# A graph layer whose messages gather rows of a table: 249 of the gathers replaced by columns copied on VectorE and ScalarE

## The chip, the cores and the metric

The kernel runs on one core of a Trainium2 chip. A core has five engines with instruction streams of their own: TensorE (PE, with its weight loads shown apart as PEld), VectorE (DVE), ScalarE (ACT), GpSimd (POOL) and SyncE (SP). PE writes its products to PSUM; the other data lie in SBUF or in device memory, between which DMA moves them. The metric is the device time of one execution in microseconds (us); less is better.

## The reference, cut to what matters

There are 12,500 nodes with 96 features (`x`) and 412,500 edges, sorted by destination. Each edge makes a message from its two ends and its own four features; messages are normalised over all edges, summed by destination, and added to a node term; a layer norm ends it.

```python
def _mlp(h, W, b, gamma, beta):
    h = relu(h @ W + b)
    mu, var = h.mean(0), square(h - h.mean(0)).mean(0)
    return gamma * (h - mu) * rsqrt(var + EPS) + beta

node_feat = _mlp(x, W_node, b_node, g_node, beta_node)
edge_feat = _mlp(edge_attr, W_edge, b_edge, g_edge, beta_edge)
message = concatenate([x[row], x[col], edge_feat], axis=1)       # 412500 x 288
message = _mlp(message, W_msg, b_msg, g_msg, beta_msg)
agg = segment_sum(message, col, num_segments=12500)
out = layernorm(x + agg + node_feat)
```

`row` is `src`, in no order; `col` is `dst`, sorted.

## The kernel before

`x[row] @ W_msg[:96]` is a row of `x @ W_msg[:96]`. So the kernel first makes that table, `p_tab`, once for all nodes (`tables`), and another, `q_tab`, for the destinations. Edges are cut into 3223 tiles of 128; four tiles are a group (`GT`), four groups a block (`BG`). There are 806 groups in 202 blocks.

The rows of `p_tab` are fetched with indirect DMAs that Pool issues: one instruction for each tile, 128 rows of 96 floats (`gather`, L207). Pool's instructions, SP's and, in the main loop, those of all engines stand in the order in which the program is written.

First stage: tables, splitting of the edge features into three bf16 parts, their statistics (`edge_norm`, on PE, ACT and DVE), and the node term (`nodes`), whose result goes to DRAM (`y0_d`). `nodes` overwrites the transposed `x` in SBUF (`xp`, 96 partitions by 12,544 nodes, the tile `big`). Meanwhile Pool gathers the rows of the first 116 groups (`SPILL`), which are written to DRAM, and then those of the next 14 groups into a ring (`RING`). In three of the first groups SP fetches the last tile's rows itself, one by one (`early_rows`, `rows_of`): it loads 16 row numbers into registers (L457) and issues a DMA for each (L461).

Main loop: 806 steps, one group each (`for k in range(last)`). `plan` spreads the 29 spilled blocks among the 173 gathered ones; a spilled block is read back whole by SP (`fetch`). In step `k`:

- DVE, `message`: h = relu(z + gathered rows), L645, z being PE's product in PSUM;
- ACT, `squared`: squares of two groups' h, each second step, L659; DVE, `moments`: adds them up, L665;
- DVE: places of the destinations as ones and zeros (`places_of`, L653), and a finished block's sums into `agg` at an address from a register (`add`, L708 and L709); registers are loaded for eight blocks at once (L698);
- PE: sums by destination (`sums`, L689), edge products for the next block (`edges`, L614), and z for the group two steps on (`linear`, L628); ACT, `prepare`: the edge products' relu, L622;
- Pool, `ahead_of`: the gathers of the group 14 ahead, four instructions, where the step's group is a gathered one;
- SP: loads for the block two ahead (`load`, `fetch`), and in steps 64 to 112 the 13 parts of the node term, back into `big` (`residual`).

For the first four blocks rows of `x` itself are gathered, and PE multiplies them (`transposed`, L633). After the loop the sums are normalised and the output made (`output`).

Of the kernel before, what the change touches and what calls it, by code (L numbers as in the profile page):

```python
# [13 lines left out]
F32 = mybir.dt.float32  # L14
BF16 = mybir.dt.bfloat16
I32 = mybir.dt.int32
U8 = mybir.dt.uint8
# [9 lines left out]
P = 128  # L27
# [36 lines left out]
RING = 14  # L64
# [7 lines left out]
CL, CE = 3, 1  # L72
BUSY = 5
# [34 lines left out]
def gnn(ctx, tc, t):  # L108
# [8 lines left out]
    lin_d = dram.tile([len(FETCHED), P], I32, name="lin_d")  # L117
    stack_d = dram.tile([HI + PLACES * BG, RL], BF16, name="stack_d")
# [5 lines left out]
    rpool = ExitStack()  # L124
    nc.sync.dma_start(src_raw, t["src"][:, :RAW * BG * GT])
    ring = rpool.enter_context(tc.tile_pool(name="ring", bufs=RING // 2))
# [90 lines left out]
    def blocks():  # L217

        waiting = []
        for b in range(SPILL // BG + BEHIND):  # L220
            if b < SPILL // BG:
                for i in range(0, BG, 2):
                    pg = ring.tile([P, 2, GT, C], F32, name="pg")
# [45 lines left out]
    with tc.tile_pool(name="win", bufs=1) as win, tc.tile_pool(name="win_ps", bufs=2, space=PSUM) as ps:  # L269
# [8 lines left out]
        nc.sync.dma_start(lin_d, lins)  # L278
        by_block = "p (b g) t -> p b (g t)"
# [202 lines left out]

    order, steps = plan()

    def fast(ring):
        y0s, pair = [], [None]

        def ahead_of(g):
            if g % 2 == 0:
                pair[0] = ring.tile([P, 2, GT, C], F32, name="pg")  # L490
            if g < NG:
                return gather(g, pair[0][:, g % 2, :, :])

        with tc.manual_schedule(engines={ET.SP, ET.Pool}):
# [9 lines left out]
            with tc.tile_pool(name="nd", bufs=1) as nd, tc.tile_pool(name="nd_ps", bufs=2, space=PSUM) as nd_ps, \  # L504
                    tc.tile_pool(name="er", bufs=2) as er, tc.tile_pool(name="es", bufs=2) as es, \
                    tc.tile_pool(name="es1", bufs=1) as es1, tc.tile_pool(name="es_ps", bufs=3, space=PSUM) as es_ps:
                node, n, extra = nodes(nd, nd_ps), 7, early_rows(er)
                for i, _ in enumerate(edge_norm(es, es1, es_ps)):
                    next(node, None)
                    if i:  # L510
                        next(extra, None)
                    while 16 * i + 150 >= 20 * n:
                        next(store, None)
                        n += 1
                for x in (node, store, extra):
                    for _ in x:
                        pass
            got = {g: ahead_of(g) for g in range(SPILL, SPILL + RING)}
        with tc.tile_pool(name="fix", bufs=1) as fix, tc.tile_pool(name="msg", bufs=2) as work, \
# [75 lines left out]

            def transposed(k):
# [27 lines left out]
            def linear(k):  # L624
                s, g = steps[k]
                n = min(GT, NT - g * GT)
                for i in range(n):
# [3 lines left out]
                                     stop=g not in raw)  # L631
# [82 lines left out]
            with tc.manual_schedule(engines={ET.SP, ET.Pool, ET.PE, ET.DVE, ET.Activation}):  # L714
# [13 lines left out]
                for k in range(last):  # L728
# [33 lines left out]
                    if k >= 64 and k % 4 == 0 and loads:  # L762
                        y0s.append(residual(loads.pop(0)))
# [223 lines left out]
    y0s, bad = fast(ring)  # L987
# [5 lines left out]
    rpool.close()  # L993
# [60 lines left out]
```

## Time and profile before

| | |
|---|---|
| median of 3 runs | 4123.67 us (4118.46 to 4125.99) |
| the profiled execution | 4123.06 us |
| its span in the profile | 4121.3 us |
| busy share PE, PEld, DVE, ACT, POOL | 64%, 54%, 38%, 27%, 75% |
| gathers (L207) | 3156 + 64, first at 3.1 us, last at 4056.4 us |
| first h of the main loop | 665.4 us |
| granted TensorE clock, mean | 0.675 |

The profile records one execution. The busy shares are means over the span; a group row gives operation, operands, shapes, count, busy time, mean duration of one, and the idle time ahead of it with what ended it. "issue" is time in which an engine waited for nothing that the profile shows. A row with a q behind the engine's name (DVEq, SPq) is an instruction that the engine's sequencer handles itself, such as the load of registers or an issued DMA. A source row gives the shortest, the median and the longest duration in ns.

### The profile page before, as it was taken

The numbers are of one execution on the slowest core, as the hardware profiler recorded it, in microseconds if no ns is written. First come the engines' busy times: TensorE is split into PE (matmuls) and PEld (weight loads), VectorE is DVE, ScalarE is ACT, GpSimd is POOL, SyncE is SP. The second block draws the span as 40 slices with busy tenths as digits, with TensorE's granted clock in tenths as the row PEclk, the third lists the DMA queues.
The fourth block names the chain that finished last, engine by engine and source line by source line (L and its number), as shares of the span: only waits on it lengthen the run. The fifth ranks groups of instructions, "written<-read, shape, count | busy, mean of one in ns | idle before, by whom it ended". The sixth has DMA issues, their size and how long they took to land.

```text
span 4121.3 us, 43082 instructions
## 1 busy us (share of the span) xinstructions
PE 2632.2 (64%) x14949; PEld 2244.2 (54%) x15169; DVE 1584.5 (38%) x3051; ACT 1123.0 (27%) x1226; POOL 3092.1 (75%) x3248
## 2 busy tenths in 40 slices
PE   4256665666666666666666666666666666666667
PEld 3012324565666656556655566655565565666656
DVE  2499995333333233322333333333233333333323
ACT  1477882222222222212222222222122222222212
POOL 7777777777777777777777777777777777777774
PEclk7667886767766666656667666666666666666665
DMA  8855662223222222222222222222222222222222
GB/s 234 279 140 123 165 161 62 60 70 77 72 50 55 59 57 58 59 54 58 56 58 58 59 47 57 60 58 55 58 59 55 58 60 56 50 59 57 58 45 64
DMA packets 214865, 317.20 MB, mean 77 GB/s; under 512 B 126498, under 2 KB 132988, under 8 KB 211808
## 3 DMA queue, kind: packets, MB, share of 16 engines
q0 software_dynamic: 103040, 158.48, 19.2%
q1 hardware_dynamic: 98635, 150.92, 12.3%
q10 hardware_dynamic: 12960, 4.93, 0.5%
q8 instruction: 122, 2.00, 0.2%
q14 instruction: 108, 0.88, 0.1%
HBM read 258.19 MB, written 55.89 MB: 76 GB/s over the span
## 4 chain that ended last, share of the span: by engine, by line
POOL 50%; issue 22%; DVE 13%; DMA 10%; PE 4%; ACT 1%; SPq 0%; POOLq 0%; another core or an unknown queue 0%; DVEq 0%; ACTq 0%
POOL pg L207 50%; DMA pg<-p_tab,src 9%; DVE estats L419 9%; PE z L628 1%; PE py L971 1%; PE pa L689 1%; DVE mixed L665 1%; DMA x<-in_ea 0%; DVE part L424 0%; DVE h L645 0%; PE pn L358 0%; DVE nstats L360 0%; DVE big L369 0%; DVE y0s L388 0%; DVE agg L394 0%
## 5 line engine op out<-in xcount | busy, mean ns | idle before, releaser
L207 POOL DMA_INDIRECT pg<-p_tab,src x3156 | 3009.5, 954 | 964.7 <-issue 919.7
L628 PE MATMUL z<-rhs,left 128*128 128x96 f32 x6446 | 1276.3, 361 | 1099.9 <-DVE h L645 1092.3
L628 PEld LDWEIGHTS z<-rhs,left 128*128 128x128 f32 x6446 | 1166.7, 267 | 1304.9 <-DVE h L645 1271.9
L645 DVE CUSTOM_DVE_ANT_0 h<-z,pg 128x384 f32<-128x384 f32 x690 | 384.1, 557 | 2301.7 <-DMA pg<-p_tab,src 2244.6
L659 ACT ACTIVATE sq<-h 128x768 f32<-128x768 f32 x404 | 339.8, 841 | 2586.6 <-DVE h L645 2577.5
L689 PE MATMUL pa<-at,h 128*97 128x80 f32 x6446 | 940.5, 307 | 4.9 <-DVE h L645 4.9
L689 PEld LDWEIGHTS pa<-at,h 128*97 128x97 f32 x6446 | 889.4, 227 | 5.9 <-DVE h L645 5.9
L665 DVE TENSOR_TENSOR mixed<-mixed,sq 128x384 f32<-128x384 f32 x802 | 449.8, 561 | 13.9
L622 ACT ACTIVATE left<-pr 127x1024 f32<-127x1024 f32 x403 | 406.8, 1009 | 90.1 <-PE pr L614 60.8
L413 PE MATMUL pr<-ea,wide 128*128 128x512 bf16 x590 | 225.5, 476 | 213.7 <-ACT r L417 135.8
L419 DVE BATCH_NORM_STATS2 estats<-r 128x6 f32<-128x512 f32 x606 | 360.9, 676 | 0.0
L417 ACT ACTIVATE r<-pr 128x1024 f32<-128x1024 f32 x303 | 307.4, 1024 | 93.0 <-DVE estats L419 65.2
L413 PEld LDWEIGHTS <-wide 128*128 128x128 bf16 x606 | 68.8, 114 | 345.9 <-issue 326.1
L614 PE MATMUL pr<-late,we 128*128 128x512 bf16 x515 | 240.6, 530 | 19.2 <-DVE at L653 15.5
L653 DVE TENSOR_TENSOR at<-rel,mixed 128x496 f32<-128x496 bf16 x202 | 135.2, 669 | 6.8
L614 PEld LDWEIGHTS <-we 128*128 128x128 bf16 x806 | 108.4, 144 | 25.2 <-issue 24.7
L207 POOL DMA_INDIRECT pg<-in_x,src_raw x64 | 60.8, 950 | 20.7 <-issue 19.2
L386 PEld LDWEIGHTS pn<-center,big 96*128 96x128 f32 x196 | 42.4, 277 | 33.0 <-DVE y0s L388 22.9
L645 DVE CUSTOM_DVE_ANT_0 h<-z,pb 128x384 f32<-128x384 f32 x100 | 52.5, 548 | 13.6 <-PE z L628 13.5
L386 PE MATMUL pn<-center,big 96*128 96x96 f32 x196 | 41.9, 358 | 17.0 <-DVE y0s L388 16.3
L191 PE MATMUL pt<-w_msg,big 96*128 96x192 f32 x196 | 37.2, 357 | 17.2 <-ACT trow L195 11.7
L709 DVE TENSOR_TENSOR agg<-pa,agg 97x79 f32 x202 | 46.5, 230 | 0.0
(125 smaller groups left out, 658.2 us busy)
## 6 DMA issues: line engine op xcount, KB each, us to landing
pg<-p_tab,src POOLq DMA_INDIRECT x3156
pb<-spill SPq DMA_DIRECT2D x29, 768.0 KB
spill<-pg SPq DMA_DIRECT2D x55, 384.0 KB
ea<-stack_d SPq DMA_DIRECT2D x25, 480.0 KB
stack_d<-y SPq DMA_DIRECT2D x24, 448.0 KB
late<-stack_d SPq DMA_DIRECT2D x57, 180.0 KB
rhs<-q_tab SPq DMA_DIRECT2D x202, 46.5 KB
x<-in_ea SPq DMA_DIRECT2D x8, 896.0 KB
```

The lines of the kernel that those rows point to most:

```text
L207: made = [nc.gpsimd.indirect_dma_start(out=pg[:, i, :], out_offset=None, in_=tab[:, :], in_offset=bass.IndirectOffsetOnAxis(ap=idx[:, i:i ...
L413: nc.tensor.matmul(pr[:, k % 2, :], wide[:, P * i:P * (i + 1)], ea[:, b % J, :], start=True, stop=True)
L417: nc.scalar.activation(r, pr, AF.Relu)
L419: nc.vector.bn_stats(stats[:, (k - o) % NS, (k - o) // NS, :], r[:, 1 - o, :])
L614: nc.tensor.matmul(prs[s, half][:, i, :], we[:, 2 * half + i, :], block[s], start=True, stop=True)
L622: nc.scalar.activation(x[:C + WN, 2 * half:2 * half + n, :], pr[:C + WN, :n, :], AF.Relu)
L628: nc.tensor.matmul(zb[k % ZB][:, i * C:(i + 1) * C], left[s % 2][:KR, g % BG, i * P:(i + 1) * P], rhs[:KR, s % RB, g % BG, :], start=True, ...
L645: nc.vector._custom_dve(TENSOR_ADD_SAT, out=h[:, :n, :], in0=z, in1=rows[:, :n, :], s0=MOST, s1=0.0)
L653: nc.vector.tensor_tensor(to, rel[:, b:b + m, :].unsqueeze(3).to_broadcast([P, m, GT, WN]), nodes_of[:, :m].unsqueeze(2).to_broadcast([P, ...
L659: nc.scalar.activation(sq[:, :m, :n, :], hb[k // 2 % HP][:, k % 2:k % 2 + m, :n, :C], AF.Square)
L665: nc.vector.tensor_tensor(wide_sq, wide_sq, sq[:, i, :, :], op=OP.add)
L689: nc.tensor.matmul(by_place[s % 2][:C + 1, :NW], hb[k // 2 % HP][:r, k % 2, t, :], at[s % AB][:r, i, o + NW * t:o + NW * (t + 1)], start=i ...
```

## The change

For three in four of the pairs of gathered groups numbered 8 to 338 (249 pairs, `COPIED`), the last tile of the pair's second group is no longer gathered. Its 128 columns of the transposed `x` are copied, one by one, from `big` to a tile of 96 x 128 (`xcs`, six of them), and PE multiplies that with `W_msg[:96]` and adds it to z. The ring slot's part for that tile is set to zero once, so `message` is as it was.

A copy moves four bytes on each of 96 partitions, at an address from a register. Numbers of the columns, times four, are made in the first stage (`cols`, `col_d`), loaded by SP for four pairs at a time (`listed`), and loaded into registers 16 at a time, one portion ahead of their use (`places_at`). Of a pair's 128 columns ACT copies 64, 80 or 80, DVE the rest (`SHARES`). At the end of each step each of the two makes one or two portions, at most 12 steps ahead of their use (`Stream`).

For this, `big` must hold `x` until the last copy. The node stage runs at double pace, `x` is loaded anew behind it (`back`), and the 13 residual loads stand in the steps behind the last copy. The ring has 16 groups in place of 14, in tiles of its own rather than from a pool, and the scratch for Pool's descriptors is set to 8192 bytes.

```diff
-RING = 14
+RING = 16
+XB = 6
+TURN = 4
+AT_A_TIME = 16
+SHARES = (64, 80, 80)
+AHEAD_BY = 12
+RATE = 0.36
+LP = (NG - SPILL) // 2
+COPIED = [q for q in range(RING // 2, LP - 6) if q % TURN != TURN - 1]
...
         def ahead_of(g):
-            if g % 2 == 0:
-                pair[0] = ring.tile([P, 2, GT, C], F32, name="pg")
+            q = (g - SPILL) // 2
+            slot = ring[q % len(ring)]
+            without = int(g % 2 and q in COPIED)
+            if without and q % len(ring) not in zeroed:
+                zeroed.add(q % len(ring))
+                nc.vector.memset(slot[:, 1, GT - 1, :], 0.0)
             if g < NG:
-                return gather(g, pair[0][:, g % 2, :, :])
+                return gather(g, slot[:, g % 2, :, :], without)
...
                 for i, _ in enumerate(edge_norm(es, es1, es_ps)):
-                    next(node, None)
+                    for _ in range(2):
+                        next(node, None)
                     if i:
                         next(extra, None)
+                    if i > 14:
+                        for _ in range(min(3, len(homes))):
+                            back(homes.pop(0))
...
+            def places_at(j, lo, hi, engine):
+                q = COPIED[j]
+                _, val = nc.values_load_multi_w_load_instructions(
+                    numbers[q // TURN % 2][:, q % TURN, lo:hi], engines=[engine], min_val=0, max_val=4 * (N - 1),
...
+            def columns(j, lo, val, engine):
+                to = xcs[j % XB].bitcast(U8)
+                for i, x in enumerate(val):
+                    a, b = to[:, 4 * (lo + i):4 * (lo + i + 1)], places_in_x[:, bass.ds(x, 4)]
+                    if engine == ET.DVE:
+                        nc.vector.tensor_copy(a, b)
+                    else:
+                        nc.scalar.activation(a, b, AF.Copy)
+            class Stream:
...
+                    self.per = RATE * len(self.parts) / len(COPIED)
...
+                def step(self, k):
+                    self.due = min(self.due + self.per, self.per + 1)
+                    while self.due >= 1 and self.done < len(self.parts):
+                        j, lo, hi = self.parts[self.done]
+                        if COPIED[j] // TURN > loaded[-1] or uses[COPIED[j]] - k > AHEAD_BY or \
+                                (j >= XB and uses[COPIED[j - XB]] >= k):
+                            break
+                        val = self.next or places_at(j, lo, hi, self.engine)
+                        self.done += 1
+                        if self.done < len(self.parts) and self.at() // TURN <= loaded[-1]:
+                            self.next = places_at(*self.parts[self.done], self.engine)
+                        columns(j, lo, val, self.engine)
+                        self.due -= 1
...
             def linear(k):
...
+                    if i == GT - 1 and copied:
+                        nc.tensor.matmul(zb[k % ZB][:, i * C:(i + 1) * C], xcs[COPIED.index(q) % XB],
+                                         w_msg[:, 0, :], start=False, stop=True)
...
                     if g >= SPILL:
                         got[ahead] = ahead_of(ahead)
                         ahead += 1
-                    if k >= 64 and k % 4 == 0 and loads:
+                    listed()
+                    for x in streams:
+                        x.step(k)
+                    if all(x.done == len(x.parts) for x in streams) and loads:
                         y0s.append(residual(loads.pop(0)))
...
-    nc = bacc.Bacc("TRN2", target_bir_lowering=False, num_devices=1)
+    nc = bacc.Bacc("TRN2", target_bir_lowering=False, num_devices=1, dynamic_dma_scratch_size=8192)
```

Pool's gathers in the middle of the loop, before; `DMASW3` and the like are the eight semaphores of Pool's own DMAs, `DVE` is the release of a ring slot:

```order
L207 DMA pg<-p_tab,src 128x96 [waits DMASW5_49,DVE_49]
L207 DMA pg<-p_tab,src 128x96 [waits DMASW6_49]
L207 DMA pg<-p_tab,src 128x96 [waits DMASW7_49]
L207 DMA pg<-p_tab,src 128x96 [waits DMASW0_49]
L207 DMA pg<-p_tab,src 128x96 [waits DMASW1_49]
L207 DMA pg<-p_tab,src 128x96 [waits DMASW2_49]
L207 DMA pg<-p_tab,src 128x96 [waits DMASW3_49]
L207 DMA pg<-p_tab,src 128x96 [waits DMASW4_49]
L207 DMA pg<-p_tab,src 128x96 [waits DMASW5_49,DVE_49]
```

The same place of Pool's stream in the change (the line is now L215, the ring's slots are named `pg_75` to `pg_82`):

```order
L215 DMA pg_80<-p_tab,src 128x96 [waits DMASW3_49,DVE_49]
L215 DMA pg_80<-p_tab,src 128x96 [waits DMASW4_49]
L215 DMA pg_80<-p_tab,src 128x96 [waits DMASW5_49]
L215 DMA pg_80<-p_tab,src 128x96 [waits DMASW6_49]
L215 DMA pg_80<-p_tab,src 128x96 [waits DMASW7_49,DVE_49]
L215 DMA pg_80<-p_tab,src 128x96 [waits DMASW0_49]
L215 DMA pg_80<-p_tab,src 128x96 [waits DMASW1_49]
L215 DMA pg_81<-p_tab,src 128x96 [waits DMASW2_49,DVE_49]
```

A pair of groups has seven gathers in place of eight, and waits for DVE once a group rather than once a pair. Each gather still waits for the one eight before it.

ACT's stream in the main loop, before:

```order
L622 ACTIVATE left_4973<-pr 127x1024
L659 ACTIVATE sq<-h_4978 128x768
L622 ACTIVATE left_4972<-pr 127x1024
L659 ACTIVATE sq<-h_4976 128x768
L622 ACTIVATE left_4972<-pr 127x1024
```

And in the change, from the activation of one step (now L713) on (`REGISTER_ALU` adds a tile's address to a column's number; 16 such pairs of rows follow a load, and some steps have a second load and 16 more):

```order
L713 ACTIVATE left_4940<-pr 127x1024
L644 TENSOR_LOAD numbers_4976
L657 REGISTER_ALU
L657 ACTIVATE xc_4971<-big 96x4
L657 REGISTER_ALU
L657 ACTIVATE xc_4971<-big 96x4
```

The next activation of this kind stands behind 33 or 66 more instructions.

DVE's stream in the change, from the places of a block on (L749, before L653); the first four rows stand there before as well, and the next h follows them there:

```order
L749 TENSOR_TENSOR at_4949<-rel,mixed 128x4x4x31
L804 TENSOR_TENSOR total<-pa_4919,total 97x1
L805 ISA
L805 TENSOR_TENSOR agg<-pa_4919,agg 97x79
L644 TENSOR_LOAD numbers_4976
L655 REGISTER_ALU
L655 COPY xc_4970<-big 96x4
L655 REGISTER_ALU
L655 COPY xc_4970<-big 96x4
```

The load and its 16 additions and copies stand between a block's sums and the next group's h (L741).

More of the change, by code (lines that the diff above doesn't have):

```diff
@@ L222, in blocks @@
                 for i in range(0, BG, 2):
[L223 removed]
+                    pg = ring[(b * BG + i) // 2 % len(ring)]
                     for k in range(2):
@@ L517, in fast @@
                         pass
+                for i in homes:
+                    back(i)
             got = {g: ahead_of(g) for g in range(SPILL, SPILL + RING)}
@@ L596, in transposed @@
+            streams = [Stream(e) for e in (ET.Activation, ET.DVE)]
             def transposed(k):
@@ L625, in linear @@
                 s, g = steps[k]
+                q = (g - SPILL) // 2
+                copied = g >= SPILL and g % 2 and q in COPIED
                 n = min(GT, NT - g * GT)
```

45 lines of the change are left out of this document (38 added, 7 removed).

## The prediction

> **What bounds the kernel now.** I read the page's shares by engine first, then the busy time by window, then the groups and waits, and last the timeline. In the first fence stand a page's row, two windows (busy us and count for PE, PEld, DVE, ACT, POOL, then granted clock, DMA share, GB/s), the gathers' group, what Pool waited for, and the two largest waits.
>
> ```profile
> PE 2632.2 (64%) x14949; PEld 2244.2 (54%) x15169; DVE 1584.5 (38%) x3051; ACT 1123.0 (27%) x1226; POOL 3092.1 (75%) x3248
> ...
> 1000.00:2000.00 1000.00, 668.98 (x4000) 607.19 (x4060) 304.17 (x649) 211.19 (x238) 756.06 (x801) 0.66 0.26 59
> ...
> 750.00:4045.00 3295.00, 2178.37 (x13096) 1970.79 (x13290) 995.24 (x2122) 689.50 (x778) 2491.41 (x2637) 0.67 0.26 58
> ...
> L207 POOL DMA_INDIRECT pg<-p_tab,src x3156: 940/945/4104, 83.4 to 4056.4; - x198
> ...
>   DVE h L645: 4.3, 14
> ...
> ACT sq L659 <- DVE h L645: 2577.5, 395, 12.4
> DVE h L645 <- DMA pg<-p_tab,src: 2244.6, 617, 8.6
> ```
>
> Pool shows only 75% busy, but it is the bound: 801 gathers in 1000 us are one each 1.2484 us, 0.945 busy and 0.30 of issue, from the first windows to 4056.4. Its wait for a free ring slot (the DVE row) is 4.3 us in all, so it never stands still for the others. DVE waits 2245 us for gathered rows, and ACT 2578 us for DVE: both have time to spare, and so has PE (2178 of 3295 us). That the consumers could go much faster shows where the ring is still full, at the loop's start:
>
> ```profile
> 668.76 0.56 DVE L645 CUSTOM_DVE_ANT_0 h<-z,pg 128x384 f32<-128x384 f32 x1 [1.15 <-PE z L628]
> ...
> 677.26 0.56 DVE L645 CUSTOM_DVE_ANT_0 h<-z,pg 128x384 f32<-128x384 f32 x1 [1.41 <-PE z L628]
> ```
>
> Five groups lie between these rows, 1.7 us each, against 4 x 1.2484 = 5.0 us for a group's gathers.
>
> **The gathers removed.** There are 345 pairs of gathered groups; numbers 8 to 338 without each fourth are 249. One gather of the pair's eight goes: 249 x 1.2484 = **311 us** off Pool. The profiled execution took 4123.06 us, 1.8 more than its span of 4121.3 and 0.6 below the runs' median of 4123.67, so it stands for them. If all that is added stays hidden: 4123.06 - 311 = 3812.
>
> The copying lies in steps 3 to 783 of 806, by the program. These 781 steps have 781 x 690/806 = 669 gathered groups: 2674 gathers or 3338 us before, 2425 or **3027 us** after. What is added must fit into 3027 us, beside the present work of these engines. The window 750 to 4045 has 2637 gathers, 659 groups or 770 steps: per step 995.24/770 = 1.29 us of DVE, 0.90 of ACT, 2.83 of PE.
>
> **ScalarE's copies.** 18,592 copies in 1,162 portions of 16, each portion with a load of 16 registers and 16 register additions. The trace has no such copy, so its price comes from its parts.
>
> ```profile
> 130.72 1.79 ACT L359 ACTIVATE agg<-pn,vec 96x512 f32<-96x512 f32 x3
> ...
> L359 ACT ACTIVATE agg<-pn,vec 96x512 f32<-96x512 f32 x24 | 15.8, 679 | 49.4 <-PE pn L358 49.4
> ...
> L659 ACT ACTIVATE sq<-h 128x768 f32<-128x768 f32 x402 | 338.9, 843 | 2578.9 <-DVE h L645 2573.3 <-DVE h L643 5.5
> ...
> L659 ACT ACTIVATE sq<-h 128x384 f32<-128x384 f32 x1 | 0.5, 523 | 4.1 <-DVE h L645 4.1
> ```
>
> 843 - 523 ns for 384 elements more is 0.83 ns each, so 203 ns are fixed and four elements take 206. Three activations of 679 that need no wait take 1.79 us, so each overlaps the next by 0.12: about **0.09 us** from copy to copy on the engine. The sequencer ahead of it must make an addition and hand out an instruction for each:
>
> ```profile
> L715 ACTq TENSOR_LOAD <-flag x1: 473/473/473, 641.1 to 641.1; - x1
> L715 SPq TENSOR_LOAD <-flag x1: 722/722/722, 650.8 to 650.8; - x1
> ...
> L698 DVEq TENSOR_LOAD <-base_at x26: 541/598/612, 678.9 to 4059.2; - x26
> ...
> L572 SPq TENSOR_LOAD <-base_at x26: 708/776/806, 655.4 to 3959.9; - x26
> ...
> L457 SPq TENSOR_LOAD <-elin x24: 1165/1226/2637, 225.2 to 598.5; - x24
> ...
> 246.45 2.81 SPq L461 DMA_DIRECT2D erow<-p_tab  x9
> ...
> L461 SPq DMA_DIRECT2D erow<-p_tab x384: 221/228/398, 226.5 to 605.0; - x192
> ...
> L709 DVEq FUSED_REGOPS  x202: 69/69/79, 679.7 to 4063.3; - x101
> ```
>
> On SP nine transfers with a register step between them take 2.81 us, 9 x 0.228 of them their own: 0.094 us for a step and the next hand-out. The dearest row is DVE's, where one step of 69 ns and its hand-out make 0.14 (next fence), up to 0.15 with rounding. I take 0.10, nearer to SP's, since one plain addition is like SP's single move; bounds 0.094 and 0.15. A load of one register takes ACT 0.473; DVE's loads go from 541 ns (two, at the end) to 598 (eight), 9.5 ns a register, which makes 0.62 for sixteen; by SP's ratio of 1226 to 722 it is 0.80. I take 0.70.
>
> ACT's sequencer: 1162 x (0.70 + 1.60) = 2673, and some 40 for its 781 large activations: **2713 us**. Its engine: 781 x 0.90 + 18,592 x 0.09 = 2376. Both are under 3027. Whether they overlap or add is told by DVE, the first three rows without a load between L653 and L708, the others with one:
>
> ```profile
> 2032.82 0.67 DVE L653 TENSOR_TENSOR at<-rel,mixed 128x496 f32<-128x496 bf16 x1
> 2033.41 0.15 DVE L708 TENSOR_TENSOR total<-pa,total 97x1 f32<-97x1 f32 x1
> 2033.48 0.23 DVE L709 TENSOR_TENSOR agg<-pa,agg 97x79 f32 x1
> ...
> 2152.68 0.67 DVE L653 TENSOR_TENSOR at<-rel,mixed 128x496 f32<-128x496 bf16 x1
> 2153.38 0.16 DVE L708 TENSOR_TENSOR total<-pa,total 97x1 f32<-97x1 f32 x1
> 2153.52 0.24 DVE L709 TENSOR_TENSOR agg<-pa,agg 97x79 f32 x1
> ```
>
> A load of 0.598 us delays L708 by only 0.11 when it is made while L653 runs: the sequencer works ahead of its engine. With that lead L709 follows in 0.07 us, without it in 0.14. In the changed order each large operation has a load right behind it, so about one load a step is covered. Only with no overlap at all would ACT need 699 + 2673 = 3372 us.
>
> **VectorE's copies.** 13,280 in 830 portions. Per copy I take 0.125 us on the sequencer, between SP's 0.094 and DVE's own 0.15 for a longer step; per load 0.8, half-way from 598 + 8 x 9.5 = 674 ns to 598 x 1226/776 = 945: 830 x (0.8 + 2.0) = 2324. The engine: 781 x 1.29 + 13,280 x 0.07 = 1937. At the dearest, 0.15 and 0.95, the sequencer takes 2781. All are under 3027; added up without overlap they would be 1007 + 2324 = 3331. A portion stands ahead of the next group's h (L645) and lasts some 2 us; h's readers are sums and squares, and behind them the ring slot's release, which the ring's slack of 16 groups x 5 us covers.
>
> **What the copies cost Pool.** The trace shows VectorE stopping a gather:
>
> ```profile
> 71.84 0.36 DVE L261 CAST part<-whole 128x384 bf16<-128x384 f32 x1 [14.99 <-DMA uses<-in_uses]
> 71.99 1.02 POOL L207 DMA_INDIRECT pg<-in_x,src_raw  x1 [0.30 <-issue]
> ...
> 644.12 1.35 DVE L533 COPY rhs<-w_e 96x1152 f32<-96x1152 f32 x1
> ...
> 645.21 0.95 POOL L207 DMA_INDIRECT pg<-p_tab,src  x1 [0.30 <-issue]
> ...
> 154.05 2.69 POOL L207 DMA_INDIRECT pg<-p_tab,src  x1 [0.30 <-issue]
> ...
> 153.89 2.02 DVE L309 TENSOR_TENSOR x<-x,y 128x1792 f32<-128x1792 f32 x1 [2.22 <-ACT y L308]
> ```
>
> The gather under L309 ends 0.83 us after it (156.74 and 155.91), the one under L261 0.81 after it; that under the copy L533 is not longer. So some DVE operations from SBUF to SBUF hold up the gather's early part until they end. If the new copies do so, a gather meets one in about 45% of the time (13,280 x 0.10 of 3027) and waits half of 0.1 us: 0.022 x 2425 = **55 us**. Bounds: 0 (as under L533), and 0.15 us for each gather that meets one, 164. I take 55, since L261 is the nearer row: a plain one-source operation with few elements.
>
> The Trainium skill's "VectorE: DVE Perf Modes" (What auto-detection actually checks) gives a copy within SBUF with an even count its two-port mode, and "SBUF — State Buffer" (SBUF: two separate sides) says that such an operation locks Pool out of the shared port for its whole length. L261 bears this out. By these pages every DVE copy here holds the port and the term is 55 or more; by L533's row alone it would be 0 and the sum 3812.
>
> **Edits at nothing.** PE gets 249 x 2 x 0.323 us = 161 us of products, 0.2 a step beside 2.83, where a step will have 3.9. Its new product waits for columns that are copied up to twelve steps ahead; behind it on PE stand sums and the next products, for which DVE's h waits, so late columns are rivals 1 and 2.
>
> ```profile
> L633 PE MATMUL z<-w_msg,xt 96*128 96x96 f32 x128 | 30.1, 323 | 6.8 <-ACT xt L604 6.8
> ...
> big<-in_xp SPq DMA_DIRECT2D x14, 336.0 KB
> ...
> big<-y_d SPq DMA_DIRECT2D x12, 384.0 KB
> ```
>
> The 14 transfers that bring x back (4.8 MB) and the doubled pace of the node stage lie in the stage before the loop, where DVE's statistics last and Pool goes on with its gathers; two more ring groups give that stage 10 us more before Pool would stand. The 13 residual loads (4.7 MB) move from steps 64 on to those behind the last copy, 20 steps or 78 us, at a DMA share of 0.26; what stands behind them on SP, the loads for two blocks ahead, has some 20 us to spare. The queue of SP gets a small load of numbers each eight groups and no wait longer than a step. Ring slots are now freed by group; the wait stays VectorE's. Together 3 us, bounds 0 and 25.
>
> **Sum:** 4123 - 311 + 55 + 3 = **3870 us**. Pool stays the bound: 3027 + 55 = 3082 us of gathers in the copying steps, against 2713 on ACT.
>
> **Rivals.**
> 1. *ScalarE becomes the bound, still a gain.* It needs more than (3082 - 40)/1162 = 2.62 us a portion: an addition and hand-out of over 0.12 us. For it speaks DVE's 0.14, against it that ACT's load is shorter than both others' and SP's 0.094. At 0.12 with loads of 0.80, 1162 x 2.72 + 40 = 3201: 119 more than Pool, **3989**.
> 2. *ScalarE is the bound and the kernel slower than before.* The point is 3338 us of ACT: 2.84 a portion, 0.134 us per copy with loads of 0.70, or loads and copies that do not overlap with the large operations (3372). At DVE's 0.15 and 0.80 it is 1162 x 3.20 + 40 = 3758, 420 over: **4543**. Against it: the lead that the sequencer showed above.
> 3. *VectorE's copies of one portion run into each other and Pool waits for the whole portion.* 2.0 us x 830 are 55% of the time, half a portion's wait is 1.0: 0.55 x 2425 = 1334, **5150**. Against it: the next operation of DVE (136.58, behind one from 134.63 to 136.65) did not hold the gather of 135.24 further, as its end shows:
>
> ```profile
> 134.63 2.02 DVE L311 TENSOR_TENSOR y<-x,y 128x1792 bf16<-128x1792 f32 x1 [1.76 <-ACT y L310]
> 135.24 2.24 POOL L207 DMA_INDIRECT pg<-p_tab,src  x1 [0.30 <-issue]
> 136.58 2.02 DVE L309 TENSOR_TENSOR x<-x,y 128x1792 f32<-128x1792 f32 x1
> ```
>
> 4. *Nothing comes of it*, because gathers are paced by rows landing and not by Pool's instructions: **4123**. Against it the even 1.248 us.
>
> **Chances.** Forecast 0.60, rival 1 0.20, rival 2 0.14, rival 3 0.02, rival 4 0.04. Faster by over 0.2% (what a measurement of this kernel can tell from no change) is the first two, 0.80; within 0.2% rival 4, 0.04; slower rivals 2 and 3, 0.16. The forecast's own range is 3805 to 3990 (port 0 to 164, the rest up to 25); for 8 in 10 it goes on through rival 1 to 4090.
>
> **What would show it.** Right: some 2971 gathers, still 0.30 us of issue between them, a mean length up by about 20 ns; ACT waiting for h some hundred us, not 2578; copies 0.09 to 0.10 us apart on ACT; PE at 70% or more. Wrong: gathers idle for h or a slot (rivals 1 and 2), ACT without waits, loads of over 0.8 us, or gathers of 1.5 us and more (rival 3).

## The result: 4055 us, where 3870 was forecast

| | before | after |
|---|---|---|
| median of the runs | 4121.07 us (4 runs, 4101.94 to 4125.99) | 4055.39 us (4 runs, 4052.78 to 4060.61) |
| ratio to before | | 0.9851 (95%: 0.9817 to 0.9884) |
| the profiled execution, its span | 4123.06, 4121.3 us | 4053.38, 4051.7 us |
| granted TensorE clock, mean | 0.675 | 0.758 |

Executions of one kernel can lie in two groups some 17 us apart (before: one at 4101.94, three from 4118.46 to 4125.99), so a difference of less than about 20 us between two kernels says little. The kernel became 1.5% faster, not 6%: 66 us of the 251 that were promised (4121 to 3870). The first fence is from the page of the changed kernel (the engines' shares; the chain that ended last; the two groups of copies); then one window of the main loop, in the columns of the prediction's windows.

```profile
PE 2504.0 (62%) x15667; PEld 2145.1 (53%) x15667; DVE 3049.6 (75%) x16338; ACT 2997.5 (74%) x19818; POOL 2851.2 (70%) x2999
...
ACT 35%; DVE 19%; issue 18%; ACTq 12%; PE 6%; DMA 5%; DVEq 3%; SPq 1%; POOL 0%; POOLq 0%
...
L657 ACT ACTIVATE xc<-big 96x4 uint8 x18592 | 1925.9, 190 | 626.1 <-issue 597.3
L655 DVE COPY xc<-big 96x4 uint8 x13280 | 1503.0, 198 | 696.9 <-issue 693.7
```

```profile
1000.00:2000.00 1000.00, 655.71 (x4330) 601.50 (x4330) 754.94 (x4712) 791.82 (x5922) 700.27 (x743) 0.76 0.25 55
```

The same row of the chain before:

```profile
POOL 50%; issue 22%; DVE 13%; DMA 10%; PE 4%; ACT 1%; SPq 0%; POOLq 0%; another core or an unknown queue 0%; DVEq 0%; ACTq 0%
```

Pool has left the chain altogether: 0%, after 50%. In 1000 us it makes 743 gathers, where it could make 801 and did so before. What it waits for now stands in the list of waits over the whole span, beside those of the other engines (engine, line, what ended the wait: us in all, times, longest):

```profile
PE pr L705 <- ACT left L713: 1030.3, 323, 6.8
...
DVE xc L655 <- issue: 693.7, 1011, 2.3
ACT xc L657 <- issue: 597.3, 1086, 1.2
...
POOL pg L215 <- DVE h L741: 242.9, 113, 15.6
...
POOL pg L215 <- DMA spill<-pg: 49.4, 7, 22.9
ACT sq L755 <- DVE h L741: 40.9, 73, 2.9
```

Pool's wait for `h` of VectorE went from 4.3 to 242.9 us: it stands for ring slots that VectorE frees too late. ScalarE waited 2577.5 us for h before and waits 40.9 now. PE waits a thousand us for ScalarE. The two copying engines hardly wait for anybody; what idle time they have is "issue", which is their own sequencers. What these do in that time shows in the instructions of the load's line and of the two copying lines (ns: least, median, longest):

```profile
L644 ACTq TENSOR_LOAD <-numbers x1162: 1011/1021/1039, 713.9 to 3965.2; - x194
L644 DVEq TENSOR_LOAD <-numbers x830: 1094/1099/1120, 715.1 to 3960.6; - x166
...
L657 ACTq ALU_OP  x18592: 35/35/53, 716.0 to 3969.5; - x200
L657 ACT ACTIVATE xc<-big x18592: 187/189/208, 716.1 to 3970.0; 96x4 uint8 x200
...
L655 DVE COPY xc<-big x13280: 155/169/427, 717.5 to 3967.4; 96x4 uint8 x199
```

A load of 16 registers takes ScalarE 1.02 us (0.70 was forecast, bounds 0.62 to 0.80) and VectorE 1.10 (0.80, bounds 0.674 to 0.945): both are over the upper bound. The timeline of ScalarE shows how they lie; here are two steps, from one `left` (L713) to the next, and the chain from 2000 to 2010 us:

```profile
2003.14 1.00 ACT L713 ACTIVATE left<-pr 127x1024 f32<-127x1024 f32 x1
2004.22 1.63 ACT L657 ACTIVATE xc<-big 96x4 uint8 x16
2005.76 0.83 ACT L755 ACTIVATE sq<-h 128x768 f32<-128x768 f32 x1
2006.89 1.63 ACT L657 ACTIVATE xc<-big 96x4 uint8 x16 [0.30 <-issue]
2009.48 1.63 ACT L657 ACTIVATE xc<-big 96x4 uint8 x16 [0.96 <-issue]
2011.02 1.00 ACT L713 ACTIVATE left<-pr 127x1024 f32<-127x1024 f32 x1
```

```profile
by line: ACT xc L657 53.2%; issue 25.7%; ACTq L644 17.8%; ACTq L657 3.5%; ACT left L713 0.5%
```

The load behind `left` (1.00 us) is hidden. The one behind `sq` (0.83 us) sticks out by 0.30. The one that stands between two portions has nothing to hide behind: 0.96 us of idle engine. The copying lasts from 716.1 to 3970.2, 3254 us or 781 steps of 4.17. ScalarE's old work (781 x 0.90 = 703), its copies (1925.9) and the idle time ahead of them (626.1) make 3255; VectorE's 1007 + 1503.0 + 696.9 make 3207. That the first sum meets the 3254 to the microsecond is partly luck, since neighbouring operations overlap: in this window ScalarE is busy for 2582.3 us and VectorE for 2472.3, which leaves ScalarE some 46 us and VectorE some 85 us of idle time that does not lie ahead of copies. So in the changed kernel both have next to no slack.

The stage ahead of the loop is longer too. The rows are the three reductions that end the edge statistics, before and after:

```profile
L424 DVE BATCH_NORM_AGGREGATE part<-estats x3: 5566/5567/5607, 622.1 to 633.1; 128x2 f32<-128x1212 f32 x3
```

```profile
L436 DVE BATCH_NORM_AGGREGATE part<-estats x3: 5567/5567/5607, 664.7 to 675.8; 128x2 f32<-128x1212 f32 x3
```

They begin 42.6 us later, and Pool stands 49.4 us (3.9 before) for ring slots whose spilling is late (the row `POOL pg L215 <- DMA spill<-pg` above).

### The profile page after: what moved, and what is told of

Read it like the earlier page. It is cut to its first block, busy times and chain, and to the rows that moved or that the text cites. A ratio compares the mean times of both kernels' runs of the same rounds, so it can differ in the third digit from the quotient of the medians.

```text
span 4051.7 us, 110364 instructions
## 1 busy us (share of the span) xinstructions
PE 2504.0 (62%) x15667; PEld 2145.1 (53%) x15667; DVE 3049.6 (75%) x16338; ACT 2997.5 (74%) x19818; POOL 2851.2 (70%) x2999
## 4 chain that ended last, share of the span: by engine, by line
ACT 35%; DVE 19%; issue 18%; ACTq 12%; PE 6%; DMA 5%; DVEq 3%; SPq 1%; POOL 0%; POOLq 0%
ACT xc L657 32%; ACTq L644 10%; DVE estats L431 7%; DVE xc L655 5%; DVEq L644 3%; DVE mixed L761 2%; PE z L721 2%; ACTq L657 2%; DVE h L741 2%; ACT left L713 1%; DMA ea<-stack_d 1%; ACT sq L755 1%; PE pr L705 1%; PE pa L785 1%; DMA q_tab<-trow 1%
## 5 line engine op out<-in xcount | busy, mean ns | idle before, releaser
L215 POOL DMA_INDIRECT pg<-p_tab,src x2907 | 2768.2, 952 | 1151.1 <-issue 790.0
L657 ACT ACTIVATE xc<-big 96x4 uint8 x18592 | 1925.9, 190 | 626.1 <-issue 597.3
L655 DVE COPY xc<-big 96x4 uint8 x13280 | 1503.0, 198 | 696.9 <-issue 693.7
L721 PEld LDWEIGHTS z<-rhs,left 128*128 128x128 f32 x6446 | 1126.4, 254 | 219.0 <-DVE h L741 133.6
L721 PE MATMUL z<-rhs,left 128*128 128x96 f32 x6446 | 1159.5, 338 | 89.1 <-DVE h L741 88.2
L785 PE MATMUL pa<-at,h 128*97 128x80 f32 x6446 | 837.7, 284 | 0.0
L785 PEld LDWEIGHTS pa<-at,h 128*97 128x97 f32 x6446 | 791.8, 205 | 0.2
L761 DVE TENSOR_TENSOR mixed<-mixed,sq 128x384 f32<-128x384 f32 x802 | 449.9, 561 | 16.3 <-ACT sq L755 2.2
L741 DVE CUSTOM_DVE_ANT_0 h<-z,pg 128x384 f32<-128x384 f32 x690 | 381.1, 556 | 76.8 <-PE z L721 52.1
L713 ACT ACTIVATE left<-pr 127x1024 f32<-127x1024 f32 x403 | 403.7, 1002 | 33.9 <-PE pr L705 33.9
L755 ACT ACTIVATE sq<-h 128x768 f32<-128x768 f32 x404 | 335.0, 829 | 43.0 <-DVE h L741 40.9
L749 DVE TENSOR_TENSOR at<-rel,mixed 128x496 f32<-128x496 bf16 x202 | 135.2, 669 | 6.8
L726 PE MATMUL z<-w_msg,xc 96*128 96x96 f32 x498 | 133.7, 364 | 0.0
L705 PE MATMUL pr<-early,we 128*128 128x512 bf16 x116 | 46.5, 493 | 117.3 <-ACT left L713 117.3
L726 PEld LDWEIGHTS z<-w_msg,xc 96*128 96x128 f32 x498 | 112.2, 277 | 0.0
L215 POOL DMA_INDIRECT pg<-in_x,src_raw x64 | 61.3, 957 | 20.7 <-issue 19.2
```

What stands on the lines that cost most here:

```text
L215: made = [nc.gpsimd.indirect_dma_start(out=pg[:, i, :], out_offset=None, in_=tab[:, :], in_offset=bass.IndirectOffsetOnAxis(ap=idx[:, i:i ...
L655: nc.vector.tensor_copy(a, b)
L657: nc.scalar.activation(a, b, AF.Copy)
L705: nc.tensor.matmul(prs[s, half][:, i, :], we[:, 2 * half + i, :], block[s], start=True, stop=True)
L713: nc.scalar.activation(x[:C + WN, 2 * half:2 * half + n, :], pr[:C + WN, :n, :], AF.Relu)
L721: nc.tensor.matmul(zb[k % ZB][:, i * C:(i + 1) * C], left[s % 2][:KR, g % BG, i * P:(i + 1) * P], rhs[:KR, s % RB, g % BG, :], start=True, ...
```

## Experiments on the loop

Theory A says that the sequencers of both copying engines are full, because of the loads. Its rivals: the copies themselves or their effect on Pool (B), ScalarE alone (C), VectorE alone (D). The first four kernels ran on one chip, where before had 4119.78; of the later ones `two_thirds_cleared` and `copies_alone` stand beside a before of 4118.82, the smaller portions beside 4119.28.

**Without the loads, on both engines.** The first portion's 16 registers serve all portions:

```diff
-                        val = self.next or places_at(j, lo, hi, self.engine)
-                        self.next = None
+                        self.next = self.next or places_at(j, lo, hi, self.engine)
+                        val = self.next
                         self.done += 1
-                        if self.done < len(self.parts) and self.at() // TURN <= loaded[-1]:
-                            self.next = places_at(*self.parts[self.done], self.engine)
                         columns(j, lo, val, self.engine)
```

> Every copy is still made, but both engines load registers for one portion only and use these 16 columns for all portions (so the copied columns are the wrong ones): 1161 of ScalarE's 1162 loads and 829 of VectorE's 830 are left out. Theory A (the sequencers of ScalarE and VectorE are both full: a load of 16 registers takes 1.02 and 1.10 us where 0.70 and 0.80 were forecast, and only about one a step is covered): without loads ScalarE needs at most 781 x 0.90 + 18,592 x 0.095 = 2469 us and VectorE 781 x 1.29 + 13,280 x 0.113 = 2508, Pool 3027; Pool is the bound again and the time is 4123 - 311 + 45 (the later start of the loop) = 3857, give or take 15. Theory B (the copies themselves, not the loads, are what does not fit, or they hold Pool up): 4000 to 4055.

Measured: **3855.0 us** (3854.45 to 3856.92), ratio 0.9368 (0.9341 to 0.9394). B falls. The loop's window has Pool back at full rate with all 31,872 copies in place:

```profile
1000.00:2000.00 1000.00, 714.80 (x4663) 646.42 (x4663) 721.54 (x5129) 811.83 (x6459) 755.86 (x802) 0.75 0.26 61
```

802 gathers, 755.86 / 802 = 0.9425 us each. The edit does one thing more than its text says: on VectorE, copies whose registers stay loaded follow each other by 0.072 us in place of 0.106 (medians; in the mean 0.091 and 0.112), some 270 us less in all, though the additions are all still made. Why is open. It does not change the reading: at the old distance VectorE would need 1007 + 13,280 x 0.112 = 2494 us (an estimate), still less than Pool's 3027. So 4055 - 3855 = **200 us** are the price of the loads.

**Without the loads, on one engine.** The same edit under `if self.engine == ET.Activation`, and under `ET.DVE`.

> As once_both, but on ScalarE alone; VectorE keeps its 830 loads. Theory A (both sequencers are full): VectorE goes on setting the pace, 4000 to 4050. Theory C (ScalarE alone is full and VectorE only waits its turn): 3857 to 3900. Theory D (VectorE alone is full): 4055, no change.

> As once_both, but on VectorE alone; ScalarE keeps its 1162 loads. Theory A (both full): ScalarE goes on setting the pace, 4000 to 4050. Theory C (ScalarE alone is full): 4055, no change. Theory D (VectorE alone): 3857 to 3900.

Measured: **3996.35 us** (0.9722, 0.9689 to 0.9755) and **4032.52 us** (0.9797, 0.9769 to 0.9826). Each frees one engine and gets 59 or 23 of the 200 us; the waits say who holds the pace then (the edits shift the line numbers a little). Without ScalarE's loads (two rows of waits):

```profile
ACT sq L760 <- DVE h L746: 729.2, 349, 5.5
DVE xc L655 <- issue: 680.7, 999, 2.3
```

Without VectorE's:

```profile
PE pr L710 <- ACT left L718: 1154.2, 326, 7.0
...
ACT xc L657 <- issue: 596.1, 1083, 1.2
DVE h L746 <- PE z L731: 360.8, 116, 7.2
DVE mixed L766 <- ACT sq L760: 360.5, 193, 3.2
...
DVE h L746 <- PE z L726: 241.6, 129, 7.6
```

In the first ScalarE waits 729 us for VectorE's h. In the second VectorE waits 361 us for ScalarE's squares and some 600 us for PE's z, and PE is the engine that waits for ScalarE. C and D fall. Two engines are within 2% of each other at the limit, and relieving one hands the pace to the other.

**Fewer columns.** Two pairs of three in place of three of four: 220 gathers removed, not 249, and 12% fewer portions.

```diff
-TURN = 4
+TURN = 3
```

> The last tile is copied in two pairs of three in place of three of four: 220 gathers fewer instead of 249, and 12% fewer portions on both engines. Theory A, C and D (the copying engines set the pace, 4.17 us a step at 1.49 portions of 2.55 us on ScalarE): a step falls to 4.17 - 0.17 x 2.55 = 3.73, 2913 us in all, below Pool's (2674 - 220) x 1.2484 = 3064; Pool binds again: 4123 - 220 x 1.2484 + 45 = 3893, faster than both kernels with fewer gathers removed. Theory B2 (what is missing was lost on Pool or in the landing of its rows): 29 gathers more, 4055 + 36 = 4091.

Measured: **3891.56 us** (3875.75 to 3901.23), ratio 0.9465 (0.9435 to 0.9495). With 29 gathers more left in, the kernel is 164 us faster than the change. What this kernel leaves out: a ring slot now changes between pairs with and without the eighth gather, and its last tile is not cleared in between, so old rows are added there. The next one clears it.

```diff
+            if g % 2 and not without:
+                zeroed.discard(q % len(ring))
             if without and q % len(ring) not in zeroed:
```

> two_thirds, in which a ring slot's last tile still held the rows of the pair gathered there before (the slots now change between pairs with and without that gather), with some 110 clearings of 128x96 on VectorE added so that the tile is zero again. They are 110 x about 0.15 us on an engine that has 12% of its copies less: Pool still binds, 3880 to 3900. If VectorE were still the bound: 3892 + 20 = 3912.

Measured: **3900.54 us** (3896.97 to 3902.89), ratio 0.949 (0.946 to 0.9519). It computes all that the reference does. Its loop is Pool's again:

```profile
1000.00:2000.00 1000.00, 645.39 (x4464) 600.52 (x4529) 750.39 (x4571) 771.44 (x5632) 755.88 (x802) 0.79 0.25 59
```

**The added work alone.** All copies, but no gather removed and the new products left out.

```diff
-            without = int(g % 2 and q in COPIED)
+            without = 0
...
-                    if i == GT - 1 and copied:
+                    if 0:
```

> All of the added work is kept, but no gather is removed: Pool gathers all eight tiles of a pair, and the products with the copied columns are left out (the copied columns are not used). Theory A (Pool is not slowed by the copies, the copying engines need 4.17 us a step): Pool's 3338 us and the copies' 3256 are near each other, 4123 + 45 = 4168, at most 4200, gathers still 0.945 us. Theory P (VectorE's copies hold the gathers up, the forecast's term of 55 to 164 us): 4223 and more, with gathers longer by 20 ns or more in the mean.

Measured: **4164.39 us** (4145.26 to 4165.53), ratio 1.0114 (1.0075 to 1.0153). Pool's window and its gathers over the run:

```profile
1000.00:2000.00 1000.00, 624.99 (x4114) 579.53 (x4176) 757.48 (x4723) 793.17 (x5938) 755.89 (x802) 0.75 0.25 58
```

```profile
L215 POOL DMA_INDIRECT pg<-p_tab,src x3156: 940/944/4138, 83.6 to 4099.4; - x198
```

802 gathers of 0.9425 us (before: 801 of 0.944), median 944 ns (945). The copies do not measurably hold up Pool; theory P falls. The 45 us that this kernel loses are those of the first stage: its edge statistics end 44.7 us later than before (the three reductions begin at 666.8 us, not 622.1).

**Smaller portions.**

```diff
-AT_A_TIME = 16
+AT_A_TIME = 8
```

> The change with portions of 8 columns: twice as many loads of 8 registers. Theory L1 (a load has a large fixed part: 8 registers take 0.60 us as in VectorE's loads of 8, so two take 1.20 where one of 16 took 1.02, and the operation a step that covers one load now covers 0.60 us instead of 0.9): ScalarE's step gets 1.49 x 0.18 + 0.35 = 0.62 us longer, 781 x 0.62 = 480, about 4530. Theory L2 (a load costs by the register, 0.51 for eight, and several can hide behind one operation): 4030 to 4100, no slower than the change.

Measured: **4182.09 us** (2 runs), ratio 1.0166 (1.0131 to 1.02). The loads:

```profile
L644 ACTq TENSOR_LOAD <-numbers x2324: 536/547/574, 715.3 to 4098.2; - x194
L644 DVEq TENSOR_LOAD <-numbers x1660: 591/595/633, 716.5 to 4095.8; - x185
```

Two loads of eight take 1.09 us on ScalarE, against 1.02 for one of sixteen, so there is little to choose by price. L1 is right in direction, but far off in size (127 us slower, not 480); on VectorE a load of eight has L1's price (0.595; 0.60), on ScalarE one between the two (0.547; 0.60 and 0.51). L2, no slower, is wrong. ScalarE's "issue" ahead of copies rose from 597 to 709 us, nearly the whole difference. I had counted cover for one load a step only; rows of this kernel show a load next to a covered one partly hidden as well:

```profile
2007.45 1.00 ACT L713 ACTIVATE left<-pr 127x1024 f32<-127x1024 f32 x1
2008.36 0.86 ACT L657 ACTIVATE xc<-big 96x4 uint8 x8
2009.41 0.87 ACT L657 ACTIVATE xc<-big 96x4 uint8 x8 [0.20 <-issue]
2010.77 0.87 ACT L657 ACTIVATE xc<-big 96x4 uint8 x8 [0.48 <-issue]
```

## Experiments on the stage before the loop

Three edits of the change could make it 43 us longer: the transfers of x (F1), the doubled pace of the node stage (F2), the numbers' preparation (F3).

```diff
-                    if i > 14:
-                        for _ in range(min(3, len(homes))):
-                            back(homes.pop(0))
...
-                for i in homes:
-                    back(i)
```

> The change without the 14 transfers that bring x back over its normalised form (the copies then move columns of the normalised x, not of x); the node stage keeps its double pace. Theory F1 (the loop starts 45 us later because these 4.8 MB stand in SP's queue ahead of the inputs of the edge statistics): the windows of 400 to 700 us show most of VectorE's lost time, so about 25 to 35 us come back: first h near 680 us, 4020 to 4030. Theory F2 (the doubled pace of the node stage): no change, 4055. Theory F3 (the numbers' two transfers at 77 to 108 us): no change, 4055.

and, in the second, also

```diff
-                    for _ in range(2):
-                        next(node, None)
+                    next(node, None)
```

> As no_back, and with the node stage at its old single pace. Theory F1: as no_back, 4020 to 4030. Theory F2: the whole 45 us come back, 4010. F1 and F2 together (VectorE lost some 15 us in 200 to 400 us, before any transfer of x): 10 to 15 us below no_back, first h at 665 to 670, 4010 to 4015. Theory F3: 4055.

Measured: **4047.88 us** (4046.27 to 4053.22) and **4021.98 us** (4019.54 to 4023.98), where the change has 4055.39 and before had 4118.82. The window of 400 to 500 us (VectorE is the third engine of the row) for before, the change, the first and the second experiment:

```profile
400.00:500.00 100.00, 66.43 (x224) 30.03 (x227) 100.00 (x172) 82.92 (x82) 75.61 (x80) 0.81 0.66 171
```

```profile
400.00:500.00 100.00, 56.75 (x214) 29.57 (x215) 82.53 (x142) 61.08 (x65) 59.44 (x63) 0.74 0.53 142
```

```profile
400.00:500.00 100.00, 55.22 (x208) 29.11 (x212) 82.49 (x141) 61.20 (x65) 58.63 (x63) 0.76 0.53 139
```

```profile
400.00:500.00 100.00, 68.90 (x220) 29.18 (x223) 100.00 (x171) 83.15 (x82) 75.62 (x81) 0.76 0.65 169
```

F1, which I held for the main cause, is worth at most 7.5 us: the change was timed in another session, and in the profiles the reductions begin only 2.0 us earlier (662.7, not 664.7). Taking the doubled pace away brings 26 more, 28.1 at the reductions, and VectorE from 82.5 to 100. That the second experiment's time lies in the range given for F1 is luck; F2, which gave it the whole 45 us, is right in kind and too large. How the pace costs this time is argued, not tested: in the changed kernel PE waits for VectorE's y0 in this stretch (`PE pn L398 <- DVE y0s L400: 34.7, 5, 7.0` over 100 to 715 us, 16.3 before), and the statistics' products stand behind these on PE. In the second experiment the reductions begin at 634.6 us, so 12.5 of the 42.6 us are left. They are there already at 100 us, where in the change VectorE waits for the numbers ahead of the eight reductions of `worst`:

```profile
96.36 0.48 DVE L289 TENSOR_SCALAR cols<-cols 101x512 int32<-101x512 int32 x1 [8.46 <-DMA cols<-in_lasts]
96.75 0.98 DVE L296 TENSOR_REDUCE worst<-rel 128x1 f32<-128x808 bf16 x1
```

**A faster version.** `two_thirds_cleared` with the single pace, all 14 transfers of x behind the statistics:

> two_thirds_cleared with the node stage at its old single pace, and all 14 transfers of x behind the statistics instead of among them (nothing is left out). Theory F2 (the doubled pace delays the statistics, and with them the loads and spills behind them in SP's queue; Pool waits 48 us for spilled slots): Pool gets about 28 us back, 3900 - 28 = 3872. Rival F1b (14 transfers in one piece, 4.8 MB or some 25 us, hold up the loop's first loads): the gain is given back, 3890 to 3905.

Measured: **3861.62 us** (3850.98 to 3872.96), ratio **0.939** (0.9365 to 0.9415). It computes everything and beats both kernels. The gain over `two_thirds_cleared` is 39 us where 28 were expected; in the profiles the reductions begin 30.1 us earlier (633.5, not 663.6). The rival falls: the transfers in one piece cost nothing that shows, for from the first of these reductions to the first h it is 43.6 us here and 43.2 before.

**The numbers.** Two tries to take F3's wait away:

```diff
-        nc.sync.dma_start(cols, ...)
-        nc.vector.tensor_scalar(cols, cols, 4.0, None, op0=OP.mult)
-        nc.sync.dma_start(col_d..., cols)
+        nc.scalar.dma_start(cols, ...)
...
+        nc.vector.tensor_scalar(cols, cols, 4.0, None, op0=OP.mult)
+        nc.scalar.dma_start(col_d..., cols)
         worst = win.tile([P, 2, BG], F32, name="worst")
```

> cleared_late with the two transfers of the columns' numbers on ScalarE's queue instead of SP's, and their product on VectorE ahead of one other operation. Theory F3 (the 12 us of the first stage that neither the transfers of x nor the pace explain come from these two transfers, 18.9 and 11.5 us of waiting, ahead of the other loads on SP's queue): 3860. Rival (they are something else, the ring's 16 groups or the order of the engines): no change against cleared_late, 3872.

```diff
         nc.vector.tensor_scalar(flag, most, 0.0, None, op0=OP.is_gt)
+        nc.vector.tensor_scalar(cols, cols, 4.0, None, op0=OP.mult)
+        nc.scalar.dma_start(col_d..., cols)
```

> cleared_late with the multiplication of the columns' numbers moved back in VectorE's order, behind the eight reductions of worst, and the store of the result on ScalarE's queue. In cleared_late_cols the multiplication still stood ahead of them and VectorE waited 20.0 us there for the numbers to land, so that run moved the wait and did not remove it. Theory F3 (VectorE's wait for the numbers, 8.5 us in the change, makes everything behind it late): the wait falls to 1 or 2 us, the statistics' reductions begin 7 to 10 us earlier (from 633.5 to about 625), Pool's time falls by as much or less: 3850 to 3860. Rival: the 12 us come from elsewhere, the reductions begin at 633 as before.

Measured: **3867.58 us** (0.9393, 0.9367 to 0.9418) and **3871.88 us** (0.9396, 0.9371 to 0.9421): no gain over `cleared_late`. Neither takes the wait away. In the first the multiplication came to stand ahead of `rel`; in the second it waits 1.19 us, and yet VectorE's work on the edge features begins late:

```profile
96.47 0.43 DVE L292 TENSOR_SCALAR cols<-cols 101x512 int32<-101x512 int32 x1 [20.04 <-DMA cols<-in_lasts]
```

```profile
113.18 2.03 DVE L321 TENSOR_TENSOR x<-x,y 128x1792 f32<-128x1792 f32 x1 [16.77 <-ACT y L320]
```

ScalarE's y in that row waits for the load of the edge features, and SP's own waits say what that load stands behind. Here are the load before, in the change and in the second try, and in the latter two what SP waited for ahead of it:

```profile
95.56 0.83 SPq L306 DMA_DIRECT2D x<-in_ea  x2
```

```profile
108.59 0.84 SPq L318 DMA_DIRECT2D x<-in_ea  x2
...
SPq L318 <- DMA col_d<-cols: 11.2, 1, 11.2
```

```profile
106.60 0.82 SPq L318 DMA_DIRECT2D x<-in_ea  x2
...
SPq L318 <- DMA col_d<-cols: 11.6, 1, 11.6
```

SP holds the load back until the store of the numbers has landed, on whichever queue that store was issued, and the load goes out 11 to 13 us later than before. The reductions begin at 633.5, 635.0 and 632.4 us in the three. So the 12 us arise before 116 us (VectorE's first operation on edge features begins at 103.2 us before, at 115.3 in the change and in the second experiment), and the trace names the wait. No run without the store was made, so that it is the only cause stays argued, and how to hide it stays open.

## Why the prediction was wrong

The runs split the miss. The forecast was 3870, with 55 for Pool's delay by the copies and 3 for the edits at nothing:

3870 - 55 (Pool is not delayed) + 40 (first stage: 3855, as `once_both` has it, less 3815) + 200 (loads) = 4055.

The 40 and the 200 are differences of measured times, so this sum had to come out; the checks on it are the 43 to 45 us by which the first stage ends later, and the loads' own prices below.

1. *What bounds the kernel* (Pool's gathers at 1.2484 us): right. With the loads out of the way the kernel takes 3855, and 4119.78 - 311 + 45 (`copies_alone`) = 3854.
2. *ScalarE's copies: the step that failed.* From copy to copy 0.095 us, forecast 0.10: right. The load was mis-sized: 0.70 forecast, 1.02 measured. I carried on the line from two to eight registers (9.5 ns each) to sixteen; from eight to sixteen it is (1021 - 547) / 8 = 59 ns each. The step stood in the prediction's own fence: SP's loads of eight took 776 ns and those of sixteen 1226, 56 ns a register, against 8 from one to eight. I used their ratio; their difference, 450 ns on top of VectorE's 598 for eight, gives 1048, near the 1099 measured. By the forecast's own sum that alone makes 1162 x (1.02 + 1.52) + 40 = 2992 us, still below 3082. What brought it to 3254 is the second half of the step: the larger of the sequencer's and the engine's sums was taken, as though they overlapped. They overlap only where a load stands behind a large operation. "About one load a step is covered" was said, but the others, one for every two steps, were then left out of the sum. In the trace of the change 469 of the 1162 portions stand right behind another one, with 0.94 us of idle engine each (442 us in all); 360 stand behind `sq` (0.30 us, 110 in all) and 324 behind `left` (0.09 us, 28 in all). Engine work and idle time add: 703 + 1926 + 626. Neither fault alone would have made ScalarE the bound: with loads of 0.70 us the idle time would shrink to some 340 us and the sum to some 2970 (an estimate, 0.32 us off each of those gaps), below Pool's 3027.
3. *VectorE's copies.* The same two faults: 1.10 us a load, not 0.80, and 3207 us in sum where 2324 were forecast for its sequencer and 3331 for no overlap at all. The copies themselves were forecast too dear: 0.125 us each, and 0.112 from one to the next in the mean.
4. *What the copies cost Pool*: forecast 55, measured 0. L261, the row that I called nearer, misled; L533, the other bound, was right. The trace of the change tests the mechanism: between 1000 and 3600 us 871 gathers begin while one of VectorE's copies runs, and they last 944 ns like the others. By the page that I had set beside it, the Trainium skill's "SBUF — State Buffer" (SBUF: two separate sides), the port pair goes to whichever starts first, and the other waits for the whole instruction. My reading of it, that "every DVE copy here holds the port" and delays gathers, is not what this trace shows.
5. *Edits at nothing*: forecast 3 (0 to 25), measured some 43. "DVE's statistics last and Pool goes on with its gathers" named the cover, VectorE's full stage, but it is no cover where the order on PE and SP changes: VectorE's share fell from 100% to 82%, and Pool stood 49 us for spilled slots. By the experiments the pace is worth 26 us, the numbers some 12 and the transfers of x at most 7.5.

Of the rivals, the first, "ScalarE becomes the bound, still a gain" (0.20), is what came, but by another way: its condition, an addition and hand-out of over 0.12 us, was not met (0.095). What happened is nearer to rival 2's second condition, loads and copies that do not overlap with the large operations, in part. Rival 1's price (3989) was too low, and it lacked that VectorE is bound as well: a cure for ScalarE alone gives 59 us. That 4055 lies inside the range of 3805 to 4090 owes something to luck, as the 55 us that Pool did not lose made up for the 43 of the first stage. (The forecast's own terms, 3812 with 0 to 164 and up to 25, reach to 4001 and not 3990.) Rival 2's point, 3338 us on ScalarE, was missed by 84 us. Rivals 3 and 4 did not come. Of the signs, 2907 + 64 = 2971 gathers, the 0.30 us between them and the 0.095 us between copies were met; PE's 70% (62%), longer gathers and ScalarE's waits for h were not. Of the signs listed as wrong three were the true ones: "gathers idle for h or a slot", "ACT without waits, loads of over 0.8 us".

## What to carry to other kernels

When work is moved from a bound engine to idle ones, count each receiving engine's time as engine work plus the loads of registers that stand between two pieces of it, not as the larger of two sums, and give cover only to those loads that stand behind an operation as long as they are. Short additions, 35 to 40 ns each here, fitted between the copies. Where two engines share the moved work evenly, they reach the limit together; then move less, since here 220 gathers gained 218 us (`two_thirds_cleared`) and 249 only 66. A stage that is called a cover must still be full after the edit: the node stage's pace, which moved no work into the loop, cost 26 us. And a store can hold back the loads behind it: here the numbers' store, which nothing needs before the loop, kept the edge features waiting for 11 us.

## What was not expected of the hardware

The time of a load of registers is no straight line in their number. On ScalarE 1, 8 and 16 take 473, 547 and 1021 ns; on VectorE 8 and 16 take 595 and 1099; on SP, in the kernel before, 1, 8 and 16 take 722, 776 and 1226. Sixteen cost nearly two loads of eight; whether the step lies right behind eight was not tried.

Where copies and gathers meet, VectorE waits here, and not Pool. In the trace of the change 14% of VectorE's copies last over 250 ns (median 169, longest 427, the row above); between 1000 and 3600 us, of those that begin 0.5 to 0.7 us after a gather's start 93% do, of those that begin at any other point hardly any. These copies end when the gather ends, to within 10 ns nearly always. So a gather holds a copy that begins in this part of its run until its own end, for up to 0.25 us, while gathers themselves keep 944 ns. That a shared port is the reason is inferred, not shown. This cost little time: a portion's sixteen copies, from the first's start to the last's, take 1.68 us in the mean, against 1.59 in the median.
